# A GNN layer on one core: where the steps of the taps' transform stand in each batch, one load asked for earlier, and the last stores on two queues

## The chip, the cores and the metric

The kernel runs on one core of a Trainium2 chip. The core has five engines that run their own instruction streams and meet at semaphores: TensorE (PE in the profile, its weight loads PEld), VectorE (DVE), ScalarE (ACT), GpSimd (POOL) and SyncE (SP). SyncE, ScalarE and GpSimd also issue DMA transfers, each in the order of its own stream. The metric is device time in microseconds of one execution; lower is better.

## The reference

Input are 32 graphs of 512 nodes with 256 features each (x) and a 512x512 adjacency per graph. A layer norm and a ReLU give h; the layer below is added to x.

```python
h = jnp.maximum(_layernorm(x), 0.0)
xc = h^T                                         # channels first
c  = relu(bn(conv1d(xc, conv1_w, 1 tap)))        # conv1
c  = bn(conv1d(c, conv2_w, 17 taps))             # conv2, along the nodes
x_conv = relu(c + xc)^T
s = h @ w_se.T + b_se                            # 3 features per node
A = exp(-dist(s, s)) * adj
x_nmp = A @ relu(h @ w_msg.T + b_msg)
# a GRU cell: inputs [x_conv, x_nmp], state h
r, z = sigmoid(...), sigmoid(...)
n = tanh(gi_n + r * gh_n)
out = x + (1 - z) * n + z * h
```

## The kernel before, in words

The 32 graphs are "batches" b in two halves (g = 0 and 1) of GB = 16. conv2 is done in the frequency domain: the nodes are cut into windows of 64, each is transformed over 80 points with a matmul (`windows_to_freq`, tile px, into xf), multiplied per frequency with the transformed taps (`product`, tile py), and transformed back much later (`inverse`). The taps' own transform is done once, in the first half: 32 steps of `weights_to_freq` (L245, tile pw). A step makes four matmuls, each of 17 rows by 80 columns over 512 elements, into four PSUM banks; They are copied into the tiles wst: the fourth by VectorE, in even steps the second too, the others by ScalarE (L262; the first two steps are ScalarE's alone). After every odd step four DMAs on SyncE's queue store wst to the DRAM tensor wd. `load_taps` (L238) brings the raw taps of four steps into one of two buffers w2p, with five DMAs on GpSimd's queue. All PSUM tiles come from one pool of eight banks.

`first_part` (L815) runs over the 16 batches of a half. Its order is written out by hand (`tc.manual_schedule`): each engine executes its instructions in the order of the program text. For one batch b of the first half that text is:

- `load_x(b + 3)` on GpSimd's queue;
- `statistics(b + 2)` (L280): mean and variance on VectorE, the reciprocal root on GpSimd (rstd);
- `transpose_h(b + 1)` (L306): eight transposes on TensorE (phT), two copies with a ReLU by VectorE into hT, a store of h to DRAM (hd) on SyncE's queue;
- `normalise(b + 2)` (L292) on VectorE;
- `between(b)` (L924): loads of the next taps in even batches, one entry of `load_weights` (L206; on SyncE's queue, the seventh, `vectors`, is GpSimd work), and the list of this batch's steps, the first in `one`, the others in `two`;
- `conv1(b)` (L319): 16 matmuls (pc), two sums by VectorE, two ReLUs by ScalarE;
- the steps in `one`; `windows_to_freq(b - 1)` with four copies by ScalarE; the steps in `two`.

The 32 steps are spread over batches 0 to 14, two each and three in batches 7 and 14. Batches 0 and 1 differ: the second step of batch 0 is kept (`last_two`) and done behind `conv1(1)`, and batch 1's own two stand around its windows. In the last batch `load_h(b0)` (L410) asks for h of batch 0 again, behind conv1; after the loop `by_chunks` (L421, ScalarE copies of hT into hq) is done for batch 15, then h of batch 1 is asked for, then come the last windows and `by_chunks` of batch 0. Behind the stage SyncE loads the first three units of transformed taps (wt, from wd), and `nodes` (L941) begins: message, affinity and aggregation per batch, starting with batch 15, with products in between. Its loop is ordered by a planner, not by hand.

The second half repeats this without the taps. Then 16 pairs of batches go through the GRU. The very last work is `last_z` (L653): the sums of the last two batches with x go out by `store` (L805), four DMAs for the first batch of the pair on SyncE's queue, and two times four for the second, alternately on SyncE's and ScalarE's queue.

Of the kernel before, what the change touches and what calls it, by code (L numbers as in the profile page):

```python
# [65 lines left out]
def gnn_layer(  # L66
# [15 lines left out]
    nc = tc.nc  # L82
# [236 lines left out]
    def conv1(b):  # L319
        H1[b] = pools["first"].tile([P, NC, D], FP, tag="h1", name=f"h1_{b}", bufs=2)  # L320
        h = N // D
        for c0 in range(0, NC, h):
            p = bank(f"pc1_{b}_{c0}").rearrange("p (c d) -> p c d", d=D)
            for j in range(h):
                c = c0 + j
                for ic in range(DC):
                    nc.tensor.matmul(p[:, j, :], HT[b][:, ic, c * P : (c + 1) * P], w1[:, ic, :],  # L327
                                     start=(ic == 0), stop=(ic == DC - 1))
            h1 = H1[b][:, c0 : c0 + h, :]
            nc.vector.tensor_add(h1, p, shift1_row[:, None, :].to_broadcast([P, h, D]))  # L330
            nc.scalar.activation(h1, h1, AF.Relu)
        if b % GB != GB - 1:
            del HT[b]
# [319 lines left out]
    def last_z(p, terms):  # L653

        d, o, ks = RZ[p], 1, range(K3)

        def gated(src, other, i, j, t=slice(0, N)):
            z, g = d[:, DC + i, j, t], DC + i
            if other is not None:
                nc.vector.tensor_add(z, other[:, t], src[:, t])  # L660
                src = z
            nc.scalar.activation(z, src, AF.Sigmoid, bias=brz[:, g : g + 1], scale=1.0)

        def places(i, t):
            return slice(t.start // 32, t.stop // 32), slice(32 * i, 32 * (i + 1))

        def turned(i, j, t=slice(0, N)):
            dst, (js, half) = d[:, i, j, t], places(i, t)
            nc.vector.tensor_mul(dst, dst, d[:, DC + i, j, t])  # L669
            if (p, j) not in OUT:  # L670
                OUT[p, j] = pools["late"].tile([P, N // 32, D // 4], FP, tag="o", name=f"o_{p}_{j}", bufs=2)
            nc.vector.transpose(OUT[p, j][:, js, half], dst.rearrange("p (j k) -> p j k", k=32))

        def added(i, j, t=slice(0, N)):
            js, half = places(i, t)
            x = XP[p][j][:, js, half]
            nc.vector.tensor_add(x, x, OUT[p, j][:, js, half])


        ts = [slice(h * N // 2, (h + 1) * N // 2) for h in range(2)]  # L680
        b1, b2, b4, *b3 = (bank(f"pz{k}_{p}") for k in range(1, 6))
        into(b1, Q1, o, ks, terms, True)
        p1 = temp("p1", f"z{p}")
        nc.scalar.copy(p1, b1)
        into(b2, Q6, o, ks, terms, True)
        u2 = temp("u2", f"z{p}")
        nc.vector.tensor_add(u2, p1, b2)
        into(b1, Q2, o, ks, terms, False)
        gated(b1, None, 0, 0)
        early_out(p, 1, 1)  # L690
        turned(0, 0)
        into(b2, Q7, o, ks, terms, False)
        u3 = temp("u3", f"z{p}")
        nc.vector.tensor_add(u3, p1, b2)
        early_out(p, 0, 1)
        added(0, 0)
        for bk, t in zip(b3, ts):
            into(bk, Q5, o, ks, terms, True, t)
            gated(bk, u3, 1, 1, t)
        into(b4, Q4, o, ks, terms, True)  # L700
        turned(1, 1)
        added(1, 1)
        gated(b4, u3, 1, 0)
        for bk, t in zip(b3, ts):
            into(bk, Q3, o, ks, terms, False, t)
            gated(bk, u2, 0, 1, t)
            if t is ts[0]:
                turned(1, 0)
        added(1, 0)
        store(p, 0, [nc.sync])  # L710
        for t in ts:
            turned(0, 1, t)
            added(0, 1, t)
            store(p, 1, [nc.sync, nc.scalar], t)
# [90 lines left out]
    def store(p, j, queues, t=slice(0, N)):  # L805
        js = slice(t.start // 32, t.stop // 32)
        for g in range(4):
            queues[g % len(queues)].dma_start(quarter(out[2 * p + j], g)[:, js], XP[p][j][32 * g : 32 * (g + 1), js])
# [6 lines left out]
    def first_part(g, freq, between, left=()):  # L815


        b0, b1 = g * GB, (g + 1) * GB
        for b in range(b0, b0 + 3):
            if b not in X and (g == 0 or b == b0):  # L820
                load_x(b)
        if g == 0:
            t = XN[b0] = pools["first"].tile([P, NC, D], FP, tag="xn", name="rows", bufs=2)
            ones, diags = t[:, 0, :P], t[:, 1:3, :].rearrange("p i (c m) -> p i c m", m=P)
            nc.vector.memset(ones, 1.0)

            for _ in range(5):
                nc.tensor.matmul(row1[1][:, : 2 * P], ident, fr.rearrange("p c g k -> p (c g k)")[:, : 2 * P], start=True, stop=True)
            batch_norm("bn1", scale1, shift1, nc.gpsimd)
            bn1_row(0, scale1, ones, diags)  # L830
            bn1_row(1, shift1, ones, diags)
        if b0 not in STATS:
            statistics(b0)
        normalise(b0)
        if g == 0:
            scale_w1()
            shift_w1()
        left = list(left)

        def fill():  # L840
            for step in left.pop(0) if left else ():
                step()

        if g > 0:
            load_x(b0 + 1)
            fill()
            load_x(b0 + 2)
        transpose_h(b0)
        fill()
        statistics(b0 + 1)  # L850
        if g > 0:
            statistics(b0 + 2)
        normalise(b0 + 1, g > 0)
        fill()
        for b in range(b0, b1):
            if b + 3 < b1:
                load_x(b + 3, nc.gpsimd)
            if b == b0:
                conv1(b)
                one, two = between(0) if g == 0 else ([], [])  # L860
                for step in one:
                    step()
                fill()
                if g == 0:
                    transpose_h(b + 1)
                    statistics(b + 2)
                    normalise(b + 2)
                else:
                    normalise(b + 2)
                    transpose_h(b + 1)  # L870
                fill()
                xf, last_two = freq(g), two
                continue
            if g == 0 and b == b0 + 1:
                conv1(b)
                for step in last_two:
                    step()
            if b + 2 < b1:
                statistics(b + 2)
            if b + 1 < b1:  # L880
                transpose_h(b + 1)
            if b + 2 < b1:
                normalise(b + 2)
            one, two = between(b - b0)
            if b > b0 + (g == 0):
                conv1(b)
            if b == b1 - 1:
                load_h(b0)
            for step in one:
                step()  # L890
            windows_to_freq(b - 1, xf)
            for step in two:
                step()
        by_chunks(b1 - 1)
        load_h(b0 + 1)
        windows_to_freq(b1 - 1, xf)
        by_chunks(b0)
        return xf
# [8 lines left out]
    with tc.tile_pool(name="freq", bufs=1) as fpool:  # L907
# [3 lines left out]
        with phase("first", "gen"):  # L911
            gen = pools["gen"]
            per = N // D
            steps = [partial(weights_to_freq, gen, pc, i) for pc in range(QI // PI) for i in range(0, PI, per)]

            X[0] = pools["first"].tile([P, NC, D], FP, tag="x", name="x_0", bufs=3)
            for c in range(NC):
                (nc.sync if c % 2 == 0 else nc.scalar).dma_start(X[0][:, c, :], x[0, c * P : (c + 1) * P, :])
            load_w1()
            load_x(1)  # L920
            load_taps(gen, 0, nc.sync)
            nc.scalar.dma_start(fwd, nc.inline_tensor(fwd_np, name="dft_fwd").ap())

            def between(b):  # L924
                if b % 2 == 0 and b // 2 + 1 < QI // PI:
                    load_taps(gen, b // 2 + 1)
                if 1 <= b <= len(load_weights):
                    load_weights[b - 1]()
                mine = spread(steps, b, GB - 1) if b < GB - 1 else []
                return mine[:1], mine[1:]  # L930

            with tc.manual_schedule():
                xf = first_part(0, freq_tile, between)

                for u in range(3):
                    load_unit(0, u)
# [156 lines left out]
```

## Time and profile before

| what | us |
| --- | --- |
| median of 4 runs | 1838.93 (1836.92, 1837.63, 1840.23, 1840.42) |
| the profiled execution | 1840.53 |
| its span, first to last instruction | 1838.7 |
| first steps of the taps' transform on TensorE | 13.67 |
| conv1 of batch 15 begins, after the last step | 156.45 |
| last windows end, first message matmul | 164.35 |
| last VectorE sum ends | 1832.46 |

The table's places are counted from the start of the span. The profile page gives busy shares by engine; a timeline lists groups of instructions with their start, their length, the engine, the line, the tile written and those read, and in brackets how long the engine had been idle and what ended that. A row `PE L255 MATMUL pw<-w2p,taps 17*80 17x512 f32 x8` is one step of the taps' transform: four fp32 matmuls, recorded as eight. In the waits, "issue" means that the engine waited for nothing the profile shows. The half-clock stretch that the windows show is told by the column PEclk, the share of full speed that TensorE's clock was granted.

### The profile page before, as it was taken

The numbers are of one execution on the slowest core, as the hardware profiler recorded it, in microseconds if no ns is written. First come the engines' busy times: TensorE is split into PE (matmuls) and PEld (weight loads), VectorE is DVE, ScalarE is ACT, GpSimd is POOL, SyncE is SP. The second block draws the span as 40 slices with busy tenths as digits, with TensorE's granted clock in tenths as the row PEclk, the third lists the DMA queues.
The fourth block names the chain that finished last, engine by engine and source line by source line (L and its number), as shares of the span: only waits on it lengthen the run. The fifth ranks groups of instructions, "written<-read, shape, count | busy, mean of one in ns | idle before, by whom it ended". The sixth has DMA issues, their size and how long they took to land.

```text
span 1838.7 us, 20108 instructions
## 1 busy us (share of the span) xinstructions
PE 1820.7 (99%) x6614; PEld 1086.9 (59%) x6614; DVE 1105.8 (60%) x2220; ACT 583.6 (32%) x1084; POOL 588.8 (32%) x572
## 2 busy tenths in 40 slices
PE   9999999999999999999999999999999999999997
PEld 6777566666997766665545554555445554555443
DVE  7775555554995555454266556654666456655666
ACT  4555443432345333333212221222212221222121
POOL 3331233334432434444331332123221323133221
PEclk9999999999999999999999999999999999999999
DMA  9999989775668987767332344224422443234412
GB/s 242 301 270 245 244 231 246 198 207 183 213 233 212 259 251 222 228 202 243 104 103 56 82 120 120 76 45 120 120 86 39 116 120 103 58 80 120 120 27 42
DMA packets 307499, 289.25 MB, mean 157 GB/s; under 512 B 148076, under 2 KB 237196, under 8 KB 307012
## 3 DMA queue, kind: packets, MB, share of 16 engines
q1 hardware_dynamic: 282436, 224.48, 46.0%
q10 hardware_dynamic: 17936, 38.42, 5.9%
q0 software_dynamic: 7024, 25.07, 4.8%
q8 instruction: 53, 0.87, 0.2%
q14 instruction: 50, 0.41, 0.1%
HBM read 191.50 MB, written 96.40 MB: 157 GB/s over the span
## 4 chain that ended last, share of the span: by engine, by line
PE 65%; issue 1%; DVE 1%; POOL 1%; ACT 0%; DVEq 0%; POOLq 0%; ACTq 0%
PE pg L601 30%; PE pn L601 15%; PE pn L491 6%; PE py L392 6%; PE pc L589 5%; PE pm L439 2%; PE pd L476 1%; PE pz L601 1%; PE psr L465 0%; DVE A L482 0%; POOL cp L579 0%; POOL nt L791 0%; POOL rz L790 0%; DVE at L481 0%; DVE rz L669 0%
## 5 line engine op out<-in xcount | busy, mean ns | idle before, releaser
L491 PE MATMUL pn<-A,msg 128*128 128x512 f32 x512 | 225.6, 593 | 0.7 <-DVE A L482 0.7
L601 PE MATMUL pg<-hp,sw 128*128 128x512 f32 x434 | 221.8, 593 | 0.7 <-DVE rz L620 0.5
L601 PE MATMUL pg<-cp,sw 128*128 128x512 f32 x434 | 221.6, 592 | 0.0
L601 PE MATMUL pg<-np,sw 128*128 128x512 f32 x434 | 221.6, 592 | 0.0
L579 POOL TENSOR_TENSOR hp<-hp 128x512 f32<-128x512 f32 x64 | 81.3, 1282 | 412.9 <-DMA hp<-hd 352.6
L371 POOL TENSOR_TENSOR both<-xf 128x256 f32<-128x256 f32 x78 | 60.6, 778 | 320.0 <-PE py L392 288.0
L491 PEld LDWEIGHTS pn<-A,msg 128*128 128x128 f32 x512 | 96.9, 190 | 110.7 <-issue 105.8
L579 POOL TENSOR_TENSOR cp<-cp 128x512 f32<-128x512 f32 x64 | 80.5, 1269 | 229.6 <-ACT cp L595 228.3
L392 PE MATMUL py<-wt,both 128*128 128x256 f32 x624 | 151.0, 384 | 0.8 <-DMA wt<-wd 0.6
L616 ACT ACTIVATE rz<-rz,brz 128x512 f32<-128x512 f32 x93 | 67.2, 724 | 260.0 <-DVE rz L620 260.0
L601 PEld LDWEIGHTS pg<-hp,sw 128*128 128x128 f32 x434 | 82.2, 190 | 104.8 <-issue 97.6
L601 PEld LDWEIGHTS pg<-np,sw 128*128 128x128 f32 x434 | 82.5, 190 | 103.8 <-issue 103.8
L601 PEld LDWEIGHTS pg<-cp,sw 128*128 128x128 f32 x434 | 82.5, 190 | 103.8 <-issue 103.8
L399 DVE TENSOR_TENSOR y<-y,py 128x256 f32<-128x256 f32 x78 | 31.8, 408 | 185.7 <-ACT y L398 181.0
L392 PEld LDWEIGHTS py<-wt,both 128*128 128x128 f32 x624 | 113.9, 190 | 43.9 <-issue 28.6
L482 DVE TENSOR_TENSOR A<-e,at 128x512 f32<-128x512 f32 x128 | 112.8, 920 | 35.4 <-ACT e L479 35.2
L358 POOL TENSOR_TENSOR wsum<-wt 128x512 f32<-128x512 f32 x78 | 109.2, 1400 | 51.4 <-DMA wt<-wd 38.3
L739 ACT ACTIVATE nt<-nt,vech 128x512 f32<-128x512 f32 x64 | 46.3, 724 | 235.7 <-DVE nt L738 235.7
L439 PE MATMUL pm<-wmsg,hq 128*128 128x259 f32 x512 | 117.6, 382 | 1.0 <-ACT hq L424 1.0
L327 PE MATMUL pc<-w,hT 128*128 128x256 f32 x512 | 116.6, 381 | 1.1 <-DVE hT L315 1.1
L601 PE MATMUL pn<-np,sw 128*128 128x512 f32 x224 | 114.4, 592 | 0.0
L601 PE MATMUL pn<-cp,sw 128*128 128x512 f32 x224 | 114.4, 592 | 0.0
(145 smaller groups left out, 2959.2 us busy)
## 6 DMA issues: line engine op xcount, KB each, us to landing
wt<-wd SPq DMA_DIRECT2D x160, 256.0 KB, 4.1
adj<-in_adj_dram SPq DMA_DIRECT2D x128, 256.0 KB, 5.4
wd<-wst SPq DMA_DIRECT2D x64, 320.0 KB, 5.2
yd<-y ACTq DMA_DIRECT2D x80, 256.0 KB, 4.1
yt<-yd SPq DMA_DIRECT2D x30, 640.0 KB, 7.4
hd<-hT SPq DMA_DIRECT2D x32, 512.0 KB, 3.9
nd<-nmp ACTq DMA_DIRECT2D x32, 512.0 KB, 4.0
xb<-in_x_dram SPq DMA_DIRECT2D x128, 128.0 KB, 3.7
```

What stands on the lines that cost most here:

```text
L327: nc.tensor.matmul(p[:, j, :], HT[b][:, ic, c * P : (c + 1) * P], w1[:, ic, :], start=(ic == 0), stop=(ic == DC - 1))
L358: nc.gpsimd.tensor_tensor(t, WT[g, u][:, 0], WT[g, u][:, 1], op=ALU.add)
L371: nc.gpsimd.tensor_tensor(both[:, 0], re, im, op=ALU.add)
L392: nc.tensor.matmul(dst, v[:, ic, :], w[:, ic, :], start=(ic == 0), stop=(ic == DC - 1))
L439: nc.tensor.matmul(p[:, : D + NS], hq[:, ic, c * P : (c + 1) * P], wmsg[:, ic, :], start=(ic == 0), stop=(ic == DC - 1))
L482: nc.vector.tensor_mul(A[b][:, mc, :], e, at)
L491: nc.tensor.matmul(p, MSG[b][:, mc, dc * P : (dc + 1) * P], A[b][:, mc, :], start=(mc == 0), stop=(mc == NC - 1))
L579: nc.gpsimd.tensor_tensor(t[:, dst, :], t[:, a, :], t[:, b, :], op=sub)
L589: nc.tensor.matmul(bk[:, t0:t1], YT[p][j][:, c, oc * P : (oc + 1) * P], back[:, n : n + t1 - t0], start=(c == 0), stop=(c == len(spans) - ...
L601: nc.tensor.matmul(bk[:, t], sw[:, k, q, o, :], terms[k][q][:, t], start=(first and i == 0), stop=(i == len(ks) - 1), skip_group_check=True)
L616: nc.scalar.activation(rz[:, g, j, :], src, AF.Sigmoid, bias=brz[:, g : g + 1], scale=1.0)
L739: nc.scalar.activation(n, n, AF.Tanh, bias=b_in[:, i : i + 1], scale=1.0)
```

## The change

Three things. In the first half's `first_part` every batch from b = 2 on now has its two steps on both sides of conv1: one behind the transposes (in batch 2 ahead of the statistics), one behind conv1. Batch 1 has only the step kept from batch 0. The 32 steps end in batch 15 rather than 14, and batches 6 and 11 have a third, behind the windows. `between` is called at the head of the batch, so `load_weights` comes ahead of the batch's store of h on SyncE's queue and, for `vectors`, ahead of the batch's rstd on GpSimd; `load_taps` becomes the head of the second slot, behind conv1 and just ahead of the second step. In the last batch `load_h(b0)` comes first, `by_chunks(15)` and `load_h(b0 + 1)` come ahead of the windows of batch 14. And the four stores of the first batch of the last pair go alternately to SyncE's and ScalarE's queue.

```diff
--- before.py
+++ after.py
@@ -707,7 +707,7 @@
             if t is ts[0]:
                 turned(1, 0)
         added(1, 0)
-        store(p, 0, [nc.sync])
+        store(p, 0, [nc.sync, nc.scalar])
         for t in ts:
             turned(0, 1, t)
             added(0, 1, t)
@@ -871,10 +871,39 @@
                 fill()
                 xf, last_two = freq(g), two
                 continue
-            if g == 0 and b == b0 + 1:
-                conv1(b)
-                for step in last_two:
-                    step()
+            if g == 0:
+
+                slots = last_two if b == b0 + 1 else between(b - b0)
+
+                def slot():
+                    for step in slots.pop(0) if slots else ():
+                        step()
+
+                if b == b0 + 1:
+                    between(b - b0)
+                    conv1(b)
+                    slot()
+                if b == b0 + 2:
+                    slot()
+                if b == b1 - 1:
+                    load_h(b0)
+                if b + 2 < b1:
+                    statistics(b + 2)
+                if b + 1 < b1:
+                    transpose_h(b + 1)
+                if b > b0 + 2:
+                    slot()
+                if b + 2 < b1:
+                    normalise(b + 2)
+                if b > b0 + 1:
+                    conv1(b)
+                    slot()
+                if b == b1 - 1:
+                    by_chunks(b)
+                    load_h(b0 + 1)
+                windows_to_freq(b - 1, xf)
+                slot()
+                continue
             if b + 2 < b1:
                 statistics(b + 2)
             if b + 1 < b1:
@@ -882,8 +911,7 @@
             if b + 2 < b1:
                 normalise(b + 2)
             one, two = between(b - b0)
-            if b > b0 + (g == 0):
-                conv1(b)
+            conv1(b)
             if b == b1 - 1:
                 load_h(b0)
             for step in one:
@@ -891,8 +919,9 @@
             windows_to_freq(b - 1, xf)
             for step in two:
                 step()
-        by_chunks(b1 - 1)
-        load_h(b0 + 1)
+        if g > 0:
+            by_chunks(b1 - 1)
+            load_h(b0 + 1)
         windows_to_freq(b1 - 1, xf)
         by_chunks(b0)
         return xf
@@ -922,12 +951,14 @@
             nc.scalar.dma_start(fwd, nc.inline_tensor(fwd_np, name="dft_fwd").ap())
 
             def between(b):
-                if b % 2 == 0 and b // 2 + 1 < QI // PI:
-                    load_taps(gen, b // 2 + 1)
                 if 1 <= b <= len(load_weights):
                     load_weights[b - 1]()
-                mine = spread(steps, b, GB - 1) if b < GB - 1 else []
-                return mine[:1], mine[1:]
+
+                n = (2, 0, *(3 if b in (6, 11) else 2 for b in range(2, GB)))[b]
+                mine = [[steps.pop(0)] for _ in range(n)]
+                if b % 2 == 0 and b // 2 + 1 < QI // PI:
+                    mine[b > 0].insert(0, partial(load_taps, gen, b // 2 + 1))
+                return (mine[0], mine[1:]) if b == 0 else mine
 
             with tc.manual_schedule():
                 xf = first_part(0, freq_tile, between)
```

## The prediction

> **What bounds the kernel now.** The page first: TensorE is busy over the whole span, so time can only come from where its work is stretched, or from the two ends where it does nothing.
>
> ```profile
> PE 1820.7 (99%) x6614; PEld 1086.9 (59%) x6614; DVE 1105.8 (60%) x2220; ACT 583.6 (32%) x1084; POOL 588.8 (32%) x572
> ```
>
> Second, the windows, cut at the events of the first half's first part, where all but the last store lies. A later pair of batches (60.67 to 79.28) runs at full clock with DMA at 0.98; the part from 25.70 to 31.95 runs at 0.52 of the clock (columns: length, busy time of PE, PEld, DVE, ACT, POOL, then clock, DMA share, GB/s).
>
> ```profile
> core 0: us, PE busy (x) PEld busy (x) DVE busy (x) ACT busy (x) POOL busy (x), PEclk, DMA share, GB/s
> 25.70:31.95 6.25, 6.25 (x26) 4.57 (x25) 2.56 (x6) 2.16 (x5) 0.64 (x1) 0.52 0.91 260
> ...
> 60.67:79.28 18.61, 18.61 (x115) 13.51 (x113) 14.92 (x41) 9.87 (x23) 6.50 (x9) 1.00 0.98 302
> ```
>
> Third, TensorE's timeline. A step of the taps' transform (L255) takes 1.10 us unhindered, its four matmuls side by side, 1.03 from its start to the next group's. The step after the windows takes 1.69, and around 22 us one takes 3.50, the windows after it 4.63 instead of 2.44.
>
> ```profile
> 22.24 3.50 PE L255 MATMUL pw<-w2p,taps 17*80 17x512 f32 x8
> 25.67 4.63 PE L342 MATMUL px<-fwd,h 128*128 128x160 f32 x16
> 30.24 1.78 PE L255 MATMUL pw<-w2p,taps 17*80 17x512 f32 x8
> ...
> 64.22 1.10 PE L255 MATMUL pw<-w2p,taps 17*80 17x512 f32 x8
> 65.25 2.44 PE L342 MATMUL px<-fwd,h 128*128 128x160 f32 x16
> 67.62 1.69 PE L255 MATMUL pw<-w2p,taps 17*80 17x512 f32 x8
> 69.24 1.09 PE L311 MATMUL phT<-ident,xn 128*128 128x128 f32 x8
> ```
>
> The weight loads say why: they wait for ScalarE's copies out of PSUM. Eight banks go round: a step (4), the windows (4), a step (4), so the second step needs the first one's banks 2.4 us after it; the copies come behind two ReLUs.
>
> ```profile
> 23.79 0.21 PEld L255 LDWEIGHTS pw<-w2p,taps 17*80 17x80 f32 x2 [0.92 <-ACT wst L265]
> 24.27 0.21 PEld L255 LDWEIGHTS pw<-w2p,taps 17*80 17x80 f32 x2 [0.27 <-ACT wst L265]
> 25.67 4.24 PEld L342 LDWEIGHTS px<-fwd,h 128*128 128x128 f32 x16 [1.19 <-ACT wst L265]
> ```
>
> Last the end: SyncE issues eight stores until 1836.03, though the last sum is ready at 1832.46; ScalarE's four are out at 1834.22.
>
> ```profile
> 1829.93 6.10 SPq L808 DMA_DIRECT2D out_dram<-xb  x8
> ...
> 1831.26 2.96 ACTq L808 DMA_DIRECT2D out_dram<-xb  x4
> ...
> 1832.03 0.43 DVE L677 TENSOR_TENSOR xb<-xb,o 128x256 f32<-128x256 f32 x1
> ```
>
> **Frame.** The profiled execution took 1840.53 us (span 1838.7 and 1.8 around it), 1.6 over the median of 1838.93. The four runs lie in two pairs (1836.92 and 1837.63, 1840.23 and 1840.42), about 3 us apart; the half-clock stretch costs about that, so perhaps not every run has it. I sum against the profiled one. No operation is added or removed.
>
> **The start, b = 1 and 2.** Batch 1 drops from three steps to one; s2 goes after windows(0), s3 behind conv1(2). Before, from the transposes of batch 2 (21.22) to the end of the step after conv1(2) and windows(1) (39.83) are 18.61 us, for groups that take 0.93 + 1.03 + 2.37 + 1.03 + 0.93 + 3.55 + 1.03 + 2.37 = 13.24 from start to start: 5.4 too long (s2 2.4, windows(0) 2.2, s3 0.7). After: windows(0) starts at 22.15; its first banks are conv1(1)'s, free at 21.97 and 22.60, its third and fourth s1's, free at 23.79 and 24.27, so it ends near 25.0. s2 waits for VectorE's hT copies (25.62) and ends near 26.7; the transposes of batch 3 wait for xn (27.07), to 27.6; conv1(2) to 31.15, s3 to 32.2, windows(1) to 34.8 (its last two banks wait 0.2 for VectorE's sums), one step more to 35.8. Gain 4.0, of which 2.9 is the half-clock stretch, if it does not come back. Weighed against the Trainium skill, "TensorE: Matmul & The Clock Gate", Part 1: it lets the clock fall after an idle window of about 3.4 us. The row differs: half clock for 6.8 us, with no idle time over 1.19 us before it; what stood there were steps whose matmuls of 17 rows ran one by one. By the rule the new order is safe; by the row s2, still spread over 1.7 us, could set it off, and the sum would be 2.9 worse.
>
> **Batches 3 to 15.** Steps now stand before and behind conv1 (3.55 us), so banks return one conv1 later. Before, the last steps exceed 1.03 per step by 0.30, 0.59, 0.18, 0.59, 0.19, 0.44, 0.82, 0.77, 0.66, 0.83, 0.67, 0.74 and -0.17: 6.6 us. What stays or is new:
> - A chain through VectorE and ScalarE: step 1.10, two VectorE copies 1.27, normalise 1.38, sums 1.29, the second ReLU 0.63, three ScalarE copies 1.58, two xf copies 0.70 is 7.95; with seven handovers of about 0.1 to 0.15 some 8.8 (an estimate), against TensorE's 8.91 per batch. In batches 3 to 6, which have the costlier side of both, 0.25 each: 1.0.
> - POOL. load_taps moves to the second slot; in batches 2, 4 and 6 it takes the buffer that the step behind it still reads, so POOL waits for that step, then issues 2.9 us of tap loads, and behind it stand load_x(b+4) and rstd(b+3). rstd still comes in time (2.5 us into the next batch, wanted at about 3). The x load lands a median 7.5 us after issue and is wanted some 6 us after: VectorE is 1 to 2 us late three times, with about 2 us of slack before the windows' banks feel it: 1.0 (0 to 4).
> - `vectors` (batch 7, some 2.4 us of POOL, waiting for its DMA, median 7.4) now stands before rstd(9): 0.5 (0 to 2).
> - Batches 6 and 11 have a third step behind the windows; its banks and the next step's are just free: 0.7 each, 1.4.
> - The eight other batches, 0.1 each: 0.8.
> - SyncE now issues load_weights before the h store; at most 4.4 us of issue, and the stores behind it have a batch to spare: 0. If that were gone, the wst buffers would stall ScalarE, a few tenths.
>
> That leaves 6.6 - 4.7 = 1.9 (bounds: 6.6 if all are covered, -2 if POOL's and the chain's ends hold).
>
> **The stage's end.** load_h(b0) stood behind conv1(15) and landed at 166.75; TensorE did not wait: from 164.35 it ran without a gap to 173.2. Gain 0 (at most 0.45, the first gap, which ends on VectorE). On the other side s31, before conv1(15)'s end at 156.45, now lies 4.7 us before the stage's end, so the last wd stores land about 3.5 us later against it and the wt and adjacency loads are issued some 2.3 later. But the DMA engines have less queued by then (first h already in, only four stores), and landings before were set by that queue: adj 7.8 us median. Cost 0, ends -0.45 and +2. The node loops behind are ordered by a planner and may shuffle: TensorE is busy 36.86 of 39.15 us from 164.35 to 203.50, so 2.3 either way; I take 0.
>
> **The last stores.** Of SyncE's eight, two go to ScalarE, which has no activation left. Six issues on each side, 0.5 us each from 1829.93, and the last pair waits for its sum (1832.46): last issue near 1833.6 instead of 1835.6. The bytes (1 MB at 200 to 250 GB/s when flowing) bound it at about 1836.3, against 1837.5: 1.0 gain (0 to 1.5). Against it speaks "DMA: Bandwidth & Descriptors", Issuing engines are not separate DMA queues: a second issuer saves only the sequencer's time, usually small. That would be a gain near 0; here that time is 6.10 us for eight, the row decides.
>
> Sum: 1840.53 - 4.0 - 1.9 - 0 - 1.0 = 1833.6 us, 0.29% under the median.
>
> **Rivals.**
> 1. *The clock falls again* at s2 near 25 us (for: it did with TensorE hardly idle; against: windows(0) then fills the window before): 1833.6 + 2.9 = 1836.5.
> 2. *Late x and POOL* (for: 6 us of lead against 7.5; DMA at 0.98 already; against: VectorE busy 14.92 of 18.61, it catches up a us per batch). The batches' gain goes: 1835.5; with their bound of -2, 1837.5.
> 3. *The chain VectorE to ScalarE becomes the bound* in all twelve batches, the other side: copies that wait behind the ReLUs and the sums behind normalise. At 10.3 us per batch instead of 9.45 it costs 12 x 0.85 = 10.2 against the start's and the end's 5.0: 1845.7. It decides from (1842.6 - 1840.5 + 5.0) / 12 = 0.6 more, a batch of 10.05. Against: the sum is 8.8.
> 4. *The steps aren't the limit*: the stretched steps only moved, as DMA at 0.93 to 0.99 paces the stage: only start's 1.1 without the clock and the end's 1.0: 1838.4.
>
> **Numbers.** Forecast 0.55, rival 1 0.15, rival 2 0.13, rival 3 0.11, rival 4 0.06. A measurement here tells about 0.2%, 3.7 us, from no change: faster is below 1835.2, slower above 1842.6. Forecast's own range 1829 to 1836 (batches' gain 6.6 below; a us or two of planner above): 0.52 of it faster, the rest within. Rivals 1, 2 and 4 give another 0.08 faster and 0.26 within. Rival 3 is slower; the planner's and chain's other mishaps 0.01 more. Together faster 0.60, same 0.28, slower 0.12. The range 1829 to 1839 takes in rivals 1, 2 and 4 and leaves rival 3 and the edges, about 0.2.
>
> **What would show it.** Right: the timeline has windows(0) directly behind the transposes near 22, clock 1.00 from 20 to 35, L255 groups of 1.1 us on both sides of conv1, batch period near 9.0, stage end near 158.5 instead of 164.35, SyncE's stores out by 1834. Wrong: rstd or stats waiting for x in batches 4, 6 and 8, L255 groups still at 1.7, waits on adj or wt from TensorE behind the stage.

## The result, and the profile after

| | before | after |
| --- | --- | --- |
| median, us | 1839.22 (60 runs, 1836.06 to 1844.81) | 1836.65 (42 runs, 1833.07 to 1844.10) |
| profiled execution, us | 1840.53 | 1838.38 |
| its span, us | 1838.7 | 1836.6 |

The ratio is 0.9989, with a 95% interval of 0.9984 to 0.9993. That is 0.11% faster (the ratio weighs all runs; the two medians alone give 0.9986): a real gain, but less than half of the 0.29% forecast, and within the 0.2% that the prediction had set as its bound for "faster". The time lies inside the predicted range, 3 us above the predicted number.

The lines that answer to those of before follow. First the busy row of the page, then two rows of the windows view (length, busy time of PE, PEld, DVE, ACT, POOL, then clock, DMA share, GB/s).

```profile
PE 1815.6 (99%) x6614; PEld 1082.5 (59%) x6614; DVE 1107.3 (60%) x2220; ACT 583.5 (32%) x1084; POOL 591.3 (32%) x572
```

```profile
25.70:31.95 6.25, 6.25 (x35) 4.59 (x34) 6.22 (x19) 2.94 (x8) 2.32 (x3) 1.00 0.92 256
75.89:93.80 17.91, 17.91 (x117) 13.00 (x113) 16.78 (x50) 10.18 (x22) 9.35 (x14) 1.00 1.00 326
```

The half clock near 25 us is gone, and a pair of batches takes 17.91 us where one took 18.61. TensorE's timeline shows why:

```profile
22.42 1.09 PE L311 MATMUL phT<-ident,xn 128*128 128x128 f32 x8
23.35 1.31 PE L342 MATMUL px<-fwd,h 128*128 128x160 f32 x8
24.99 1.35 PE L342 MATMUL px<-fwd,h 128*128 128x160 f32 x8 [0.32 <-ACT wst L265]
26.27 1.57 PE L255 MATMUL pw<-w2p,taps 17*80 17x512 f32 x8
...
64.72 1.10 PE L255 MATMUL pw<-w2p,taps 17*80 17x512 f32 x8
65.75 3.72 PE L327 MATMUL pc<-w,hT 128*128 128x256 f32 x16
69.40 1.10 PE L255 MATMUL pw<-w2p,taps 17*80 17x512 f32 x8
70.43 2.44 PE L342 MATMUL px<-fwd,h 128*128 128x160 f32 x16
```

The windows of batch 0 stand directly behind the transposes, and from batch 4 on nearly all steps take 1.10 us, on both sides of conv1. The exceptions are three steps ahead of conv1, with 1.21, 1.26 and 1.62 us in batches 10, 12 and 13; the one in batch 3 takes 1.62 too. The end of the span:

```profile
1828.14 4.94 SPq L808 DMA_DIRECT2D out_dram<-xb  x6
...
1828.15 5.03 ACTq L808 DMA_DIRECT2D out_dram<-xb  x6
...
1830.24 0.42 DVE L677 TENSOR_TENSOR xb<-xb,o 128x256 f32<-128x256 f32 x1
```

All stores are issued by 1833.2, 2.5 us after the last sum, and the span ends 5.9 us after it; before it was 6.3.

**Where the time went.** The execution is cut at four events of the timeline: the transposes of batch 2, the first message matmul (end of the stage), the transpose of the features behind the second aggregate, and the end of the last VectorE sum. "Half clock" is the time in which the granted clock was 0.50, without the idle end of the span, which every execution has. All in us.

| execution | to batch 2 | stage | behind it | to last sum | tail | half clock | span |
| --- | --- | --- | --- | --- | --- | --- | --- |
| before | 21.2 | 143.1 | 46.0 | 1622.1 | 6.3 | 6.8 | 1838.7 |
| after | 22.4 | 136.4 | 49.3 | 1622.6 | 5.9 | 3.4 | 1836.6 |
| difference | +1.2 | -6.7 | +3.3 | +0.5 | -0.4 | | -2.1 |

The 1.2 us ahead of batch 2 come with the first loads, which the change doesn't touch; in the other profiled executions this stretch was 21.5 to 23.7 us, and 23.3 in experiment 1, which has the kernel before's code there. The stage gained 6.7 us, more than forecast; half of the 6.8 us at half clock, 3.4 us, is part of that. Half of the gain was lost directly behind the stage. TensorE there, before:

```profile
183.49 7.03 PE L491 MATMUL pn<-A,msg 128*128 128x512 f32 x16
...
194.64 3.77 PE L439 MATMUL pm<-wmsg,hq 128*128 128x259 f32 x16 [0.98 <-ACT hq L424]
```

and after:

```profile
167.15 1.33 PE L476 MATMUL pd<-sr,sl 9*128 9x512 f32 x8 [0.62 <-ACT sr L467]
...
180.28 7.13 PE L491 MATMUL pn<-A,msg 128*128 128x512 f32 x16 [2.01 <-ACT e L479]
...
195.80 1.13 PE L476 MATMUL pd<-sr,sl 9*128 9x512 f32 x4 [0.68 <-ACT e L479]
196.86 3.44 PE L392 MATMUL py<-wt,both 128*128 128x256 f32 x8
```

The aggregate waits 2.01 us for an exponential, and the products at 196.86 run at half clock (3.44 us; the same group takes 1.99 in other executions). The exponential itself waits for a buffer that VectorE's product with the turned adjacency empties, and VectorE waits for the adjacency's load:

```profile
177.72 1.31 DVE L481 STREAM_TRANSPOSE at<-adj 128x512 f32<-128x512 f32 x2 [2.35 <-DMA adj<-in_adj_dram]
```

SyncE's queue tells why it is late. The stage ends at 158.81; the last wd stores stand 3.5 us ahead of that and land at 162.47, the wt units wait for them, and the adjacency is queued behind the wt units. Before, with the stage's end at 164.35:

```profile
153.12 7.83 SPq L269 DMA_DIRECT2D wd<-wst  x8
161.05 3.22 SPq L412 DMA_DIRECT2D hT<-hd  x2
165.13 2.71 SPq L354 DMA_DIRECT2D wt<-wd  x6
167.95 10.16 SPq L408 DMA_DIRECT2D adj<-in_adj_dram  x8
```

and after:

```profile
155.28 2.87 SPq L269 DMA_DIRECT2D wd<-wst  x4
158.26 2.99 SPq L412 DMA_DIRECT2D hT<-hd  x2
162.54 2.69 SPq L354 DMA_DIRECT2D wt<-wd  x6
165.34 7.87 SPq L408 DMA_DIRECT2D adj<-in_adj_dram  x6
```

Against the stage's end the first two of the last four wd stores land at -0.5 and +0.8 us (before -3.1 and -1.8), the first wt is issued at +3.7 (before +0.8), and the adjacency of batch 15 lands at +18.8 (before +15.2). The very last wd store can't be compared: before, the trace has no landing for it.

### The profile page after: what moved, and what is told of

Read it like the earlier page. It is cut to its first block, busy times and chain, and to the rows that moved or that the text cites. A ratio compares the mean times of both kernels' runs of the same rounds, so it can differ in the third digit from the quotient of the medians.

```text
span 1836.6 us, 20110 instructions
## 1 busy us (share of the span) xinstructions
PE 1815.6 (99%) x6614; PEld 1082.5 (59%) x6614; DVE 1107.3 (60%) x2220; ACT 583.5 (32%) x1084; POOL 591.3 (32%) x572
## 4 chain that ended last, share of the span: by engine, by line
PE 65%; issue 1%; DVE 1%; POOL 1%; ACT 0%; DVEq 0%; POOLq 0%; ACTq 0%
PE pg L601 30%; PE pn L601 15%; PE pn L491 6%; PE py L392 6%; PE pc L589 5%; PE pm L439 2%; PE pd L476 1%; PE pz L601 1%; PE psr L465 0%; DVE A L482 0%; POOL cp L579 0%; POOL nt L791 0%; POOL rz L790 0%; DVE at L481 0%; DVE rz L669 0%
```

## The experiments

All were timed against the kernel before on the same chip, five rounds each. Two theories stand against each other throughout: that the stage's gain is what the prediction says (steps too close in PSUM banks) and the loss behind it comes of the late wd stores; and that the gain or the loss is of something else (ScalarE's order, the clock, h, the planner).

**1. The last stores alone.**

```diff
 # before.py
-        store(p, 0, [nc.sync])
+        store(p, 0, [nc.sync, nc.scalar])
```

> Kernel before with one edit: the last pair's first half is stored over SyncE and ScalarE in turn. In the changed kernel the time from VectorE's last sum to the span's end fell from 6.3 us to 5.9 only, where the prediction had 1.0. Theory (the stores' data, not their issue, sets the end): all issues are out about 2.5 us after the last sum instead of 3.6, the end comes 5.9 us after it, so 0.3 to 0.4 us less than before, a ratio of 0.9998. Rival (the issue time sets the end, and the changed kernel's tail was spoilt by something else): 5.2 us from the last sum to the end, 1.0 us less, a ratio of 0.9994.

Measured: 1837.57 us, ratio 0.9994 (0.9985 to 1.0002). From the last sum to the end 5.93 us. The time alone can't tell 0.4 from 1.0 us, but the tail can: 5.93 is what the theory has, and the rival's 5.2 is out. In the ten profiled executions with these stores on both queues the tail is 5.8 to 6.2 us, in the two without (before and experiment 4) 6.3 and 6.4. With both queues issuing, six issues take 4.93 us on SyncE, 0.82 us each with the gaps between them, and the last store lands 2.5 us after its issue; before, the last one landed 1.9 us after it.

**2. The adjacency ahead of the wt units.**

```diff
 # after.py
                 xf = first_part(0, freq_tile, between)
-                for u in range(3):
-                    load_unit(0, u)
...
             load_adj(todo[0])
             with tc.manual_schedule():
+                if g == 0:
+                    for u in range(3):
+                        load_unit(0, u)
                 begin(0)
```

> Changed kernel, but batch 15's adjacency is asked for ahead of the first three wt units, which wait for the last wd stores. Theory (behind the stage VectorE waits for this adjacency: 2.35 us at L481, and through the exponentials and products TensorE loses 3.3 us up to the second aggregate): the four adjacency loads are issued near 161, land some 5 us sooner, VectorE's wait on adj goes, and from the first message matmul to the second aggregate it takes 39 to 40 us instead of 42.4; 2.5 to 3.3 us less than the changed kernel, near 1833.5. Rival (the loss is of the clock and of the planner's order, and the adjacency is late without cost): VectorE's wait goes but the 42 us stay, 1836 to 1837. Rival 2 (the products then wait for the wt units, asked for some 2 us later): a wait of TensorE on wt or wsum of 1 to 2 us takes its place.

Measured: 1838.79 us, ratio 0.9997 (0.9988 to 1.0005), so the change's gain is gone. The adjacency was issued at 160.8 to 162.4, but landed only at 173.9, 15.6 us after the stage's end, and the first wt units at 175.0 to 179.5. Two lines of the waits from 158 to 180 (in total, count, longest, us):

```profile
DVE at L481 <- DMA adj<-in_adj_dram: 7.0, 1, 7.0
...
PE py L392 <- DMA wt<-wd: 5.9, 1, 5.9
```

The swap put a worse wait in the place of the first, as rival 2 had it but of 5.9 us instead of 1 to 2, and the theory's "VectorE's wait goes" failed: the planner also placed VectorE's turning of the adjacency earlier, so it waited longer. The adjacency landed 3.2 us sooner against the stage's end than in the changed kernel, and the wt units later; that both share the same bandwidth (the DMA share is 0.94 over the 52.4 us behind the stage) would explain it, but no run shows it. Half clock came behind the idle TensorE too:

```profile
166.55:169.96 3.41, 1.98 (x13) 0.98 (x13) 0.46 (x5) 2.19 (x5) 0.00 (x0) 1.00 1.23 193
169.96:173.38 3.42, 0.00 (x0) 0.00 (x0) 0.00 (x0) 1.09 (x3) 0.00 (x0) 0.50 1.11 206
```

**3. The loads of h where they were.**

```diff
 # after.py
-                if b == b1 - 1:
-                    load_h(b0)
                 if b + 2 < b1:
                     statistics(b + 2)
...
                     conv1(b)
+                    if b == b1 - 1:
+                        load_h(b0)
                     slot()
-                if b == b1 - 1:
-                    by_chunks(b)
-                    load_h(b0 + 1)
...
-        if g > 0:
-            by_chunks(b1 - 1)
-            load_h(b0 + 1)
+        by_chunks(b1 - 1)
+        load_h(b0 + 1)
```

> Changed kernel with the loads of h at the stage's end as in the kernel before: h(0) asked for behind conv1(15), h(1) behind the last batch. It tells apart two reasons for the late adjacency: in the changed kernel the load of h(2) went ahead of wt and adjacency on SyncE's queue (some 1.3 us of the delay of 3.6), and the last wd stores come later against the stage's end (some 2.3). If it is the first, from the first message matmul to the second aggregate it takes about 40.5 to 41 us instead of 42.4 and the time falls by 1 to 2 us; if it is the second, it stays at 42 to 43 us and the time is the changed kernel's within 1 us, or up to 1 us worse since h(0) and h(1) come later.

Measured: 1837.01 us, ratio 0.9989 (0.9981 to 0.9997), the changed kernel's. It doesn't tell the two reasons apart as meant: the load of h(2) stayed ahead of the wt units (it is placed by the planner, so it doesn't come of the place of h(0) and h(1)). It shows something else. Its profiled execution had no half clock, and behind the stage it took 47.6 us: so of the 3.3 us that the changed kernel lost there, about 1.7 are its half-clock stretch and 1.6 are waits. And undoing the h part alone changed nothing that can be measured.

**4. The first step ahead of conv1, nothing else.**

```diff
 # before.py
+            if g == 0 and b > b0 + 1:
+                for step in one:
+                    step()
+                one = []
             if b > b0 + (g == 0):
                 conv1(b)
```

> Kernel before with one move: from batch 2 on the first step of the batch stands ahead of conv1, and the second stays behind the windows. Theory (a step is stretched to 1.69 us because its PSUM banks come round too soon, with only the windows between it and the step before; conv1 between the two gives 3.55 us more): the second steps fall from 1.69 to about 1.10 us, the batch period from about 9.45 to 9.0, and the stage ends 4 to 6 us sooner than 164.35, with start and half clock about as before; 1834 to 1835.5. Rival (ScalarE's order of copies stretches the step, wherever its banks are from): second steps stay at 1.6 to 1.7 and the time at 1839 within 1 us.

Measured: 1835.89 us, ratio 0.9982 (0.9972 to 0.9992), with the slow start and its half clock (6.8 us) still there. TensorE in a batch:

```profile
68.29 1.10 PE L255 MATMUL pw<-w2p,taps 17*80 17x512 f32 x8
69.32 1.09 PE L311 MATMUL phT<-ident,xn 128*128 128x128 f32 x8
70.34 1.38 PE L255 MATMUL pw<-w2p,taps 17*80 17x512 f32 x8
71.65 3.72 PE L327 MATMUL pc<-w,hT 128*128 128x256 f32 x16
75.21 2.34 PE L342 MATMUL px<-fwd,h 128*128 128x160 f32 x16
```

The step behind the windows, 1.69 us before, takes 1.10 although it stands where it stood: the step whose banks it needs is now one conv1 further ahead, and that step's copies leave ScalarE before the ReLUs instead of behind them. This one move changed both the distance in banks and ScalarE's order, so it doesn't tell which of the two shortened the step. The first step, with only the transposes between it and the step before, takes 1.3 to 1.65 us in batches 2 to 7 and 1.1 to 1.4 later. The stage is 139.5 us, 3.6 less; the steps end with batch 14 here, and behind the stage it takes 45.0 us, with nothing lost.

**5. The changed kernel with all steps done by batch 14.**

```diff
 # after.py
-                n = (2, 0, *(3 if b in (6, 11) else 2 for b in range(2, GB)))[b]
+                n = (2, 0, *(3 if b in (4, 7, 10, 13) else 2 for b in range(2, GB - 1)), 0)[b]
```

> Changed kernel, but the 32 steps end with batch 14: a third step in batches 4, 7, 10 and 13, none in batch 15. Theory (behind the stage the changed kernel loses 1.6 us to waits, since the last wd stores and with them wt and the adjacency come later against the stage's end; in the run with the first step ahead alone, whose steps end with batch 14, that stretch took 38.2 us): the last wd store lands before the stage's end, the waits of TensorE ahead of the first aggregate (1.3 to 2.0 us) go, and from the first message matmul to the second aggregate it takes 38 to 39.5 us instead of 40.8 (without half clock). The stage itself stays at 135 to 136.5 us from the transposes of batch 2, up to 2 us more if third steps stall on the wst buffers. Time 1834.5 to 1836. Rival (the loss is of the stage's shorter end, whatever the stores do: h and the messages come sooner than adjacency can): 40.5 us or more stay and the time is the changed kernel's or worse.

Measured: 1829.88 us, ratio 0.9954 (0.9942 to 0.9966): better than both kernels, by 9.3 us than before and 6.8 than after, and 4.6 us under the expected range. The stage is as long as expected, 135.0 us; behind it, 43.35. SyncE's queue and the windows row of the stretch behind the stage, which ends at 157.33 here:

```profile
148.18 2.88 SPq L269 DMA_DIRECT2D wd<-wst  x4
151.16 4.77 SPq L412 DMA_DIRECT2D hT<-hd  x2
156.11 2.69 SPq L354 DMA_DIRECT2D wt<-wd  x6
158.91 10.34 SPq L408 DMA_DIRECT2D adj<-in_adj_dram  x8
```

```profile
157.33:200.68 43.35, 43.00 (x181) 28.65 (x180) 29.81 (x84) 21.91 (x45) 13.14 (x14) 1.00 0.94 240
```

The third of the last four wd stores lands at 153.97, 3.4 us ahead of the stage's end (the fourth has no landing in the trace), the first wt is issued 1.2 us ahead of that end, the adjacency of batch 15 lands at +13.6 us, VectorE doesn't wait for it, and TensorE is busy 43.00 of 43.35 us. The theory holds, and the stores' lateness was worth more than the 1.6 us of waits: the changed kernel's profiled execution is 6.0 us slower in this stretch, 1.7 of it clock. Four of the five runs had a mean clock of 0.998, which in the profiled executions means no half clock outside the idle end, or one stretch and a short idle end; of the changed kernel's 42 runs it was 13.

**6. The third steps in other batches.**

```diff
 # after.py
-                n = (2, 0, *(3 if b in (6, 11) else 2 for b in range(2, GB)))[b]
+                n = (2, 0, *(3 if b in (3, 6) else 2 for b in range(2, GB)))[b]
```

> Changed kernel with its two third steps in batches 3 and 6 instead of 6 and 11. Theory (the 1.6 to 2 us lost in batch 12 come of two sets of wd stores in one batch, when the eight wst buffers aren't out yet): the stall at batch 12 goes; in batch 6, which now has two sets, a stall of 0 to 2 us comes in its place, less if the queue is shorter there. Stage 134 to 136 us against 135.1 to 136.4, the rest as in the changed kernel: 1835 to 1837. Rival (DMA's backlog grows to the stage's end wherever the third steps are): the wait on wst stays in batches 11 to 13 and the stage is as long.

Measured: 1837.90 us, ratio 0.9995 (0.9986 to 1.0003); stage 136.2 us. The changed kernel's waits from 100 to 135 had

```profile
DVE wst L263 <- DMA wd<-wst: 4.7, 3, 1.8
...
ACT wst L265 <- DMA wd<-wst: 2.6, 4, 1.1
```

and its batch 12 took 10.52 us instead of 8.96. Here batch 12 takes 8.96, with no wait on wd there, and the wait stands in 70 to 90 instead, behind batch 6, which now has two sets of stores:

```profile
ACT wst L265 <- DMA wd<-wst: 2.2, 1, 2.2
...
DVE wst L263 <- DMA wd<-wst: 1.1, 1, 1.1
```

It costs one batch period of 10.39 instead of 8.96, 1.4 us. So here the stall follows the batch with two sets of stores, not the stage's end; the time, a little above the expected range, gained nothing by it. It isn't in every execution: in experiments 2 and 3, whose steps stand as in the changed kernel, batch 12 took 9.17.

**7 and 8. The new start with older batches behind it.** In 7, one step ahead of conv1 and one behind the windows, in 8 none ahead; both have third steps in batches 3, 5, 8 and 11 and end with batch 14.

```diff
 # after.py, both
-                n = (2, 0, *(3 if b in (6, 11) else 2 for b in range(2, GB)))[b]
+                n = (2, 0, 2, *(3 if b in (3, 5, 8, 11) else 2 for b in range(3, GB - 1)), 0)[b]
 # 7
                     conv1(b)
-                    slot()
+                    if b == b0 + 2 or len(slots) > 1:
+                        slot()
 # 8
-                if b > b0 + 2:
-                    slot()
...
                 windows_to_freq(b - 1, xf)
-                slot()
+                while b > b0 + 1 and slots:
+                    slot()
```

> The start of the changed kernel (batches 1 and 2), then the order of the run with the first step ahead alone: one step ahead of conv1, one behind the windows, third steps in batches 3, 5, 8 and 11 behind conv1, none in batch 15; loads of h and last stores as in the changed kernel. If the gains add, the stage is the 139.5 us of that run less the start's 4.0 (2.9 of it half clock), 135 to 136 us, the stretch up to the second aggregate 38 to 39.5 us, and the time 1832 to 1834, better than both kernels by 2 to 4 us. Rival (what the start gains is lost later, since the steps put off must fit into the batches behind): stage 137 to 139 us and 1835 to 1837.

> The start of the changed kernel alone: batches 1 and 2 as in it, then both steps behind conv1 and behind the windows as in the kernel before, third steps in batches 3, 5, 8 and 11, none in batch 15 (loads of h and last stores as in the changed kernel). By the prediction's term the start is worth 4.0 us: from the transposes of batch 2 to those of batch 4 no half clock, the later second steps at 1.7 us as before, stage 138.5 to 139.5 us instead of 143.1, time 1835 to 1836. Rival (the start only moves the stall, and the steps put off cost what it saves): stage 141 us or more and a time above 1837.

Measured: 1845.29 us, ratio 1.0032 (1.0020 to 1.0043), and 1844.31 us, ratio 1.0031 (1.0019 to 1.0043). Both are slower than before, but not for the reason that the rivals named. In 8 the waits from 80 to 92 are a chain from GpSimd to TensorE:

```profile
POOL vech L158 <- DMA vec<-in_vecs_dram: 6.3, 2, 5.7
DVE xn L303 <- POOL rstd L290: 4.4, 1, 4.4
...
PE px L342 <- DVE h L330: 3.5, 1, 3.5
```

`vectors` waits for its load with the next rstd queued behind it on GpSimd; the load had been asked for a batch earlier, at 73.9 to 76.8 us, and landed at 81.2 to 82.7. In the same place the clock fell for 6.8 us. In 7 the same wait costs VectorE 2.7 us, and later the taps come late, since `load_taps(7)` in batch 12 leaves them 6 us:

```profile
143.02 2.34 PE L255 MATMUL pw<-w2p,taps 17*80 17x512 f32 x8 [3.65 <-DMA w2p<-in_w2T_dram]
```

What the start is worth can still be read from 8: from the transposes of batch 2 to conv1(3) it takes 14.8 us with two steps, before 20.86 with four; at 1.03 a step that is 4.0 us. But the 20.86 us hold the half clock of that one execution: in experiment 1, with the same code there and half clock for 3.4 us of it instead of 6.8, it is 19.26, and the start is worth 2.4 us.

**9. Experiment 5 with the loads of h where they were** (the edits of 3 and of 5 together).

> As the run whose steps end with batch 14 (1829.88 us), but with the loads of h where the kernel before has them: h(0) behind conv1(15), h(1) behind the last batch. Theory (asking for h sooner is worth nothing by itself, as in the changed kernel, where undoing it left the stretch behind the stage at 47.6 us either way): from the first message matmul to the transposes behind the second aggregate 43.3 to 44 us, time 1829.5 to 1831. Rival (with the stores out in time, the sooner h is what saves the 0.98 us that TensorE waited on hq in the kernel before): that wait comes back, 44.5 to 45.5 us, time 1831 to 1832.5.

Measured: 1833.64 us, ratio 0.9964 (0.9951 to 0.9977). The rival was right: the wait that the kernel before has is back, and behind the stage it takes 44.5 us instead of 43.35.

```profile
186.22 3.77 PE L439 MATMUL pm<-wmsg,hq 128*128 128x259 f32 x16 [0.98 <-ACT hq L424]
```

The same wait of 0.98 us stands in all four profiled executions with h asked for as before and the wd stores out in time (before, 1, 4 and 9), and in none of the four with h sooner (5, 7, 8 and 10). So h sooner is worth about 1 us of trace, once the wd stores are out in time; where they weren't, experiment 3 shows no gain. The medians differ by 3.8 us, of five runs each; the intervals overlap, and the trace's 1 us is the safer figure. Experiments 3 and 9 differ in nothing but the place of the steps, and neither profiled execution has half clock: 47.6 us behind the stage with steps in batch 15, 44.5 without, so 3.2 us is what the late stores cost there.

**10. Experiment 8 with `vectors` a batch later.**

```diff
 # the kernel of experiment 8
         load_vectors,
+        lambda: None,
         vectors,
```

> As the run with the start alone (1844.31 us), but the second batch-norm's vectors on POOL one batch later (batch 8 instead of 7), so that their load has landed. In that run POOL waited 5.66 us for it with rstd of batch 9 queued behind, VectorE 4.40 for rstd, TensorE 3.51, and the clock fell for 6.83 us. Theory (that wait alone made the start look bad): no wait of POOL on vec, stage 139 to 141 us instead of 146.6, no half clock near 88, time 1836.5 to 1839. Rival (the steps put off don't fit behind conv1 and the windows): the batches stay at 9.9 to 11 us from batch 3 on and the time above 1840.

Measured: 1836.24 us, ratio 0.9982 (0.9973 to 0.9991), 8.1 us less than in 8. The wait on vec with rstd behind it is gone, and the stage is 141.3 us: so that wait, with the clock that fell behind it, had made most of the start's bad look. The rival had a part too. Batches 4 and 5 took 10.9 us, and where two steps stand side by side behind the windows they stretch. In batch 11 the clock fell behind such a pair, though not behind one about as long in batch 5:

```profile
124.41 3.26 PE L256 MATMUL pw<-w2p,taps 17*80 17x512 f32 x16
```

(The line numbers are one higher in this kernel.)

**All together**, cut as in the table above (us; profiled executions):

| execution | stage | behind it | half clock | median | ratio |
| --- | --- | --- | --- | --- | --- |
| before | 143.1 | 46.0 | 6.8 | 1839.22 | 1 |
| after | 136.4 | 49.3 | 3.4 | 1836.65 | 0.9989 |
| 1 last stores | 141.5 | 44.8 | 6.8 | 1837.57 | 0.9994 |
| 2 adjacency first | 136.2 | 52.4 | 10.2 | 1838.79 | 0.9997 |
| 3 h as before | 135.1 | 47.6 | 0 | 1837.01 | 0.9989 |
| 4 first step ahead | 139.5 | 45.0 | 6.8 | 1835.89 | 0.9982 |
| 5 steps end in 14 | 135.0 | 43.4 | 0 | 1829.88 | 0.9954 |
| 6 thirds in 3 and 6 | 136.2 | 49.5 | 6.8 | 1837.90 | 0.9995 |
| 7 second behind windows | 149.3 | 44.2 | 13.7 | 1845.29 | 1.0032 |
| 8 start alone | 146.6 | 44.7 | 6.8 | 1844.31 | 1.0031 |
| 9 as 5, h as before | 135.0 | 44.5 | 0 | 1833.64 | 0.9964 |
| 10 as 8, vectors later | 141.3 | 44.1 | 3.4 | 1836.24 | 0.9982 |

Every kernel whose steps end in batch 14 takes 43.4 to 46.0 us behind the stage, every one whose steps end in 15 takes 47.6 or more. VectorE's wait for the adjacency of batch 15 goes with it: 2.35 us in the changed kernel, 7.0, 1.5 and 2.4 in experiments 2, 3 and 6, and none in the other eight executions.

## Why the prediction was right or wrong

The time fell into the range partly by luck: the stage gained more than forecast, the stretch behind it lost what the sum had put at 0, and the two partly cancelled. With half clock taken off on both sides (half of its length, an estimate) the stage gained 3.3 us, the stretch behind it lost 1.6 and the tail gained 0.4. That is 2.1 us, near the 2.0 us that a ratio of 0.9989 stands for, where the sum had 6.9.

**The start: the size was right, its worth in the median was not.** The term was 4.0 us. Experiment 8 gives 4.0; the changed kernel's own trace 3.4 (16.46 us to conv1(3) with three steps). But 2.9 of the 4.0 was the half-clock stretch, taken out of the one profiled execution as if every run had it. Of 53 runs of before that stood beside experiments 1 to 8, 19 had a mean clock of 0.998, little or no half clock; 18 had 0.997, 15 had 0.996 and one 0.995. Of the changed kernel's 42 it was 13, 18 and 9. The change removed half clock near 25 us, and half clock came up elsewhere about as often. At clock 0.998 the two kernels' means are 1837.7 and 1835.0, 2.7 us apart, hardly another gap than the medians' 2.6: the clock gave the median next to nothing. The frame had a hint of this (two pairs of runs 3 us apart), and the sum did not use it.

**Batches 3 to 15: too low.** The term was 1.9; measured from conv1(3) to the stage's end it is 122.3 before and 119.9 after, with one step more to do: 3.4, and 4.7 in experiment 3, which has the same order. Of the five deductions, four cost nothing or little in the changed kernel's execution: no batch was longer for the chain through VectorE and ScalarE (8.96 us in batches 3 to 5), the late x (VectorE waited 1.35 us in batch 4) was swallowed, `vectors` cost nothing, and the third steps of batches 6 and 11 stretched their batches by 0.15 and 0.31 beyond their own 1.03. What cost time was the one thing priced at zero: the wst buffers, "a few tenths", took 1.6 us in batch 12. Experiment 2 shows that the x term was no phantom, since there x(8) came 2.7 us late and cost 1.2 us, and experiment 8 that `vectors` can cost 4.4 us of VectorE's time, above the bound of 2.

**The stage's end: this step failed.** The prediction saw that the last wd stores would land some 3.5 us later against the stage's end (2.6, by the first two of the four) and the wt and adjacency loads go out 2.3 later (2.9 for the first wt), and then wrote "Cost 0, ends -0.45 and +2", because the DMA engines would have less queued. It cost 3.3 us in the profiled execution: 1.6 of waits, and 1.7 of a half-clock stretch that followed them. The execution of before is the slowest of three with its code there (46.0 us; experiments 1 and 4 took 44.8 and 45.0), so the loss was rather more than less. The queue was not emptier where it counted: the adjacency of batch 15 landed 7.9 to 9.0 us after issue, where the same four loads had taken 7.6 to 8.3. Experiment 5 moves only the steps back into batch 14 and gets the whole stretch back, and 2.7 us more than before, 1 us of it by the sooner h.

**The planner: 0, right.** TensorE's order behind the stage is the same in both kernels; only the load of h(2) moved ahead of the wt units.

**The last stores: the mechanism right, the size not.** 1.0 forecast, 0.4 measured (experiment 1 the same). The sum counted 0.5 us per issue, though the row of before that it went by, 6.10 us for eight, says 0.76 with the gaps; with both queues they took 0.82, and the last store landed later after its issue. What the Trainium skill says in "DMA: Bandwidth & Descriptors", Issuing engines are not separate DMA queues, that a second issuer saves only the time on the sequencer and that this is usually small, came nearer to the measured 0.4 us than the row did.

**The rivals.** *The clock falls again*: it did, but at 197 us instead of 25, and its number, 1836.5, was met by a sum of other terms. *Late x and POOL*: seen in experiment 2, hidden in the changed kernel. *VectorE to ScalarE as the bound*: no, the period is 8.96 and not 10. *DMA paces the stage*: no, at a share of 1.00 it moved 326 GB/s where it had moved 302.

Of the signs named, windows behind transposes, clock 1.00, steps of 1.10 us on both sides, a period near 9.0 and the stage's end near 158.5 (158.81) came as written. The sign against, waits behind the stage, came too, on VectorE's side: TensorE's own wait is put down to an exponential.

## What to carry to other kernels

A step that is moved later takes its stores with it: follow them to the first load that reads what they wrote, and to whatever is queued behind that load; here steps that ended one batch later lost behind the stage 3.3 of the 6.7 us that their better places had earned in it, and ending them a batch sooner made the kernel 0.46% faster than before instead of 0.11%. A stretch of half clock in one profiled execution is not a cost that a change will remove until the clocks of its other runs have been counted. And an engine that waits for a load holds up all that is queued behind it, so put such work where the load has long been in.

## What the runs showed of the hardware

**In ten of twelve falls the clock fell after a window with little full-height matmul work, idle or not.** In all executions the clock changes on a grid of 3.41 us that starts elsewhere each time. The window ahead of the changed kernel's stretch, and the stretch:

```profile
193.84:197.25 3.41, 2.73 (x12) 0.96 (x11) 3.41 (x15) 2.10 (x5) 0.79 (x1) 1.00 1.23 199
197.25:200.67 3.42, 3.42 (x10) 2.71 (x9) 3.42 (x6) 2.23 (x5) 0.71 (x2) 0.50 1.16 218
```

TensorE was busy for 2.73 us of that window by the profile, but only 0.62 of it with matmuls over 128 rows; the rest were those of 9 rows (pd). I counted the same for every window of full clock in the twelve profiled executions, apart from the first 15 us and the idle end. Ten times the clock fell; the window ahead had 0.00, 0.00, 0.44, 0.46, 0.62, 0.76, 0.90, 0.97, 1.01 and 1.33 us of full-height matmuls. It kept after every window with more than that. Below, it kept after several with 0.97 to 1.33 us, and 14 to 16 few-row matmul records reached into each of these, where the ones that fell had up to 8, but for one with 0.44 us. That reads as a count of array activity in which few-row matmuls weigh little, with a limit near 40% of the window (1.33 of 3.41 is 39%); no run varied it by itself, so it stays an inference. Two falls near 11 us (10.73 and 11.29, experiments 1 and 6) do not fit: their windows had 2.2 and 2.4 us, much of it transposes. The Trainium skill, in "TensorE: Matmul & The Clock Gate", Part 1, has the free-running window of 3413 ns, which agrees with the grid of these traces, and its table of the two states puts the fall behind an idle window; here eight of the ten came with TensorE partly or wholly busy in that window.

**This explains part of the spread of the runs.** A stretch of 3.41 us costs 1.7, and whether a low place of the program falls into one window or two depends on the grid's start. The means by clock of the changed kernel, 1835.0 at 0.998, 1836.6 at 0.997 and 1839.0 at 0.996, stand 1.6 and 2.4 apart. It is not all: at 0.998 alone these runs reach from 1833.1 to 1837.2, and in experiment 6 the four runs at 0.998 were slower than the four at 0.997 (means 1838.2 and 1836.4).
